# A graph layer on one core: sixteen groups of the first norm ahead of the tables with eight load buffers, the densest groups in twos, the last layer's dense pair due 100 slots before its end

## The chip, the cores and the metric

The kernel runs on one core of a Trainium2 chip. The metric is the device time of one execution in microseconds (us), and shorter is better. Before the change three runs gave 6620.86, 6623.79 and 6653.34 us, a median of 6623.79. One further execution was taken by the profiler; all durations below come from it.

## The reference

There are 12500 nodes with 256 features each and 200000 edges (`src`, `dst`), sorted by `dst`. `dst` is drawn as a square of a uniform number, so that low nodes have many edges. Cut to what matters:

```python
xn = layernorm(x)
h = xn
for l in range(3):                        # three graph layers
    s = segment_sum(h[src], dst); cnt = segment_sum(1, dst)
    h = (s / max(cnt, 1)) @ Wl[l].T + bl[l] + h @ Wr[l].T
    h = leaky_relu(h, 0.01) if l < 2 else log_softmax(h)
x = x + h + linear_attention(xn)          # 4 heads of 32
t = layernorm(x)                          # top 2 of 8 experts, softmax router
out = x + t + sum(comb[:, e] * (gelu(t @ w1[e] + b1[e]) @ w2[e] + b2[e]) for e in range(8))
```

Every layer therefore needs the complete result of the layer before, since an edge may start at any node.

## The kernel before, in words

**Tiling.** The nodes are cut into 98 blocks of 128 (`NB`). Blocks are numbered from the end by `r`: r = 97 is block 0, the one with the most edges. The list `falling` holds groups of consecutive blocks in the order in which they are worked, from r = 0 up: 23 groups of four (`G`), then r 92 to 95 as one group of four and r 96 to 97 as one of two, 25 in all. `FEWER` is 92, `MORE` is 96. The edges of a block are cut into slots of at most 128 edges; a table `due` gives the slot at which block r is complete at the latest, 1240 for r = 91 and 1404 for r = 95.

**The start** (L275 to L604). Instructions of this part are placed by a scheduler that goes by data dependences and gives priority to what the program writes earlier. (1) Edge numbers are loaded in chunks into `val`, whether they are sorted is tested, and `val` is written to a table `edges` in device memory (L411). (2) `first_norm` (L279) normalizes one group: load `xt` on SP's DMA queue (L176), statistics on DVE (L228, L229), a root on ACT (L231), the norming on ACT (L289), a store to `y` on ACT's DMA queue (L291). The first `EARLY` = 10 groups are written ahead of the test and the write of `edges`, the other 15 behind the tables. Four buffers hold loads (`xt`), three hold results (`o_norm`). (3) The tables say for each slot which nodes its 128 edges start at (`src_of`) and which node of the block they end at (`dst_of`): samples of `edges` (L427), a gather `near` (L444), the slot ends, `pack` for the three densest pairs of blocks with 33 comparing passes each (`junk`, L532), and 13 rounds that gather 128 edge rows, turn them on TensorE and copy them (L577 to L601, tile `got`, two buffers).

**The three layers** (`on_the_way`, L1072). From here on the order of instructions is the order in which the program writes them. In layers 0 and 1 each slot has a gather by POOL of 128 rows of `y` (L1380), a one-hot matrix made by DVE for four slots at a time (L1372), and a matmul on TensorE that adds one-hot x messages to the block's sums in `acc` (L1399). When a block's slots are over, `take_up` (L1410) scales its sums on DVE and clears them; when the last block of a group is taken up, the group's `products` (L669) are queued: in layer 0 its transposes (`turned`, L661 and L663) and the product with Wl (`p_l`, L679), then transposes and the linear step of the next layer (`linear`, L240: `p_mm` L247, additions L257, for layer 2 also the three bf16 parts L268 and L269, stores of `y` and `z`). The six densest blocks, r 92 to 97, take no slots in layers 0 and 1: a count matrix of each pair of blocks, made in layer 0, is multiplied with all rows of `y` (`sums`, L1308, matmul L1330), spread evenly up to slot `sums_to`. Layer 2 does so only for r 96 and 97 (`LAST` = 1); the other blocks have slots there, and messages travel as three bf16 parts, three matmuls per slot.

`load_z` (L1451) brings a group's half-made `z` of the next sum. It lies in one of three buffers `h` of four blocks; only the last group, of two blocks, has a buffer `h_c` of its own in layers 0 and 1.

**Experts in layer 2.** When a group has its sums, DVE finishes `z`, SP stores it (L1448), and the group is `ready`. `softmaxed` (L807) loads it again (L812, L814), takes log-softmax (maximum L819, exponentials and logarithm on ACT), the norm (L228 to L237), transposes (L661), the router (L847), the top two and `comb` (to L879), its transpose (L883) and the product with `b2` (L892). `expert_steps` (L908) runs the eight experts of a group (`p_h` L975, Gelu L977, `p_y` L944, weighing L931), and between these steps lets the next ready group's `softmaxed` go on one step, once the group before has been stored (L902). The steps are let in slot by slot by a credit in the loop of `on_the_way_of` (L1351): 1.12 us per slot, less 0.6 for each step of `sums`. What is left when the slots are over runs after them, in the same order.

Of the kernel before, what the change touches and what calls it, by code (L numbers as in the profile page):

```python
# [41 lines left out]
F32 = mybir.dt.float32  # L42
# [13 lines left out]
P = 128  # L56
D = 256
# [5 lines left out]
G = 4  # L63
# [2 lines left out]
RING, SHARED = (4, 6, 4), (1, 2, 2)  # L66
W = D + 1
AHEAD = 8
EARLY = 10
MSGS, PARTED = 32, 24  # L70
FEW = 4
HOTS = 3
# [1 line left out]
PAIRS = 3  # L74
# [12 lines left out]
def gps_kernel(ctx: ExitStack, tc: tile.TileContext, x, src, dst, wlr, bl, wq, wk, wv,  # L87
# [4 lines left out]
    NB = (N + P - 1) // P  # L92
# [6 lines left out]
    FEWER = NB - DENSE  # L99
    MORE = NB - 2 * LAST  # L100
    falling, group_of = [], []
    for r0, r1 in ((0, FEWER), (FEWER, NB)):
        for r in range(r0, r1, G):
            n = min(G, r1 - r)
            group_of.extend([len(falling)] * n)
            falling.append((NB - r - n, n))
    NG = len(falling)
# [62 lines left out]
    def rows(t, b, n):  # L170

        return t[b * P:(b + n) * P, :].rearrange("(j p) d -> p j d", p=P)

    def load_x(t, b, n):
        if b + n < NB or tail == P:
            nc.sync.dma_start(t[:, :n, :], rows(x, b, n))  # L176
            return
        nc.vector.memset(t, 0.0)
        if n > 1:
            nc.sync.dma_start(t[:, :n - 1, :], rows(x, b, n - 1))  # L180
        nc.sync.dma_start(t[:tail, n - 1, :], x[N - tail:N, :])
# [41 lines left out]
    def norm_stats(pool, t, n):  # L223

        st = pool.tile([P, G, nc.vector.BN_STATS_DIM], F32, name="st")
        mv = pool.tile([P, G, nc.vector.BN_AGGR_DIM], F32, name="mv")
        for j in range(n):
            nc.vector.bn_stats(st[:, j, :], t[:, j, :])  # L228
            nc.vector.bn_aggr(mv[:, j, :], st[:, j, :])  # L229
        rs = pool.tile([P, G], F32, name="rs")  # L230
        nc.scalar.activation(rs[:, :n], mv[:, :n, 1], AF.Sqrt, bias=eps)  # L231
        return mv, rs
# [41 lines left out]
    with ExitStack() as first:  # L274
        sort = first.enter_context(tc.tile_pool(name="sort", bufs=1))  # L275
        work = first.enter_context(tc.tile_pool(name="work", bufs=2))
        psum = first.enter_context(tc.tile_pool(name="psum1", bufs=1, space=PSUM))

        def first_norm(b, n):  # L279
            xt = work.tile([P, G, D], F32, name="xt", bufs=4)  # L280
            load_x(xt, b, n)
            o = work.tile([P, G, D], F32, name="o_norm", bufs=3)
            mv, rs = norm_stats(work, xt, n)
            nc.vector.reciprocal(rs[:, :n], rs[:, :n])
            less = work.tile([P, G], F32, name="less_mean")
            nc.vector.scalar_tensor_tensor(less[:, :n], mv[:, :n, 0], -1.0, rs[:, :n],
                                           op0=OP.mult, op1=OP.mult)
            for j in range(n):
                nc.scalar.activation(o[:, j, :], xt[:, j, :], AF.Identity, bias=less[:, j:j + 1],  # L289
                                     scale=rs[:, j:j + 1])  # L290
            nc.scalar.dma_start(rows(y_tab[0], b, n), o[:, :n, :])  # L291
# [111 lines left out]
        for t, w in ((wq_sb, wq), (wk_sb, wk), (wv_sb, wv), (wo_sb, w_out)):  # L403
            nc.scalar.dma_start(t, w)
        for b, n in falling[:EARLY]:
            first_norm(b, n)
# [18 lines left out]
        for c in range(KC):  # L425
            n = min(P, NK - c * P)
# [57 lines left out]
        for s0 in range(0, NS, 512):  # L484
            n = min(512, NS - s0)
# [116 lines left out]

        for b, n in falling[EARLY:]:
            first_norm(b, n)  # L604
# [467 lines left out]
    def on_the_way():  # L1072


        with ExitStack() as stack:
# [14 lines left out]
            with ExitStack() as two:  # L1090
                msgs = take_messages(open_pool(two, "messages"), MSGS)
                for layer in range(2):
                    with ExitStack() as own:
                        psum = open_pool(own, f"psum_w{layer}", space=PSUM)
                        on_the_way_of(layer, tables[layer], due[FEWER - 1], work, psum, inv, msgs,
                                      a, Counts(own), None)
# [6 lines left out]
            c = Counts(stack)  # L1103
            c.work = open_pool(stack, "sums2")
            on_the_way_of(2, where, due[MORE - 1], work, psum, inv, msgs, a, c, e)

    class Counts:
# [243 lines left out]
    def on_the_way_of(layer, table, last, work, psum, inv, msgs, a, c, e):  # L1351
# [7 lines left out]
        hots, made_of, cleared, taken, zs, at, at_of = {}, {}, {}, {}, {}, (), -1  # L1359
# [90 lines left out]

        def load_z(g):  # L1451
            b, n = falling[g]
            if g == NG - 1 and not e:
                zs[g] = c.work.tile([P, G, D], F32, name="h_c")
            else:
                zs[g] = work.tile([P, G, D], F32, name="h", bufs=3)
            nc.sync.dma_start(zs[g][:, :n, :], rows(z_tab[layer], b, n))

        def ask(g):

            while layer == 0 and g not in made:
                stage(1)
            load_z(g)
# [47 lines left out]
        n_steps = (LAST if e else PAIRS) * (NB + 6) + 3  # L1511
        if layer == 0:
            counting = c.all_counted(psum, whole, inv)
        sums_to = last - 40
        due_steps, done_steps = 0.0, 0
        credit, r, g = 0.0, 0, 0
        nc.vector.memset(acc, 0.0)
# [138 lines left out]
```

## Time and profile before

| what | value |
|---|---|
| runs | 6620.86, 6623.79, 6653.34 us (median 6623.79) |
| profiled execution, its own time | 6628.48 us |
| its span (1.8 us less) | 6626.7 us |
| granted TensorE clock, mean | 0.903 |
| busy: TensorE, weight loads | 5213.0 us (79%), 3776.3 us |
| busy: VectorE (DVE), ScalarE (ACT), GpSimd (POOL) | 2590.6, 1025.2, 4076.9 us |
| start, to the first gather of layer 0 | 202.4 us |
| last gather of layer 0, first of layer 1 | 2472.3, 2514.5 us |
| last gather of layer 1, first of layer 2 | 4323.7, 4350.5 us |
| last product of a slot, end | 6527.4, 6626.7 us |

How to read it: the page cuts the span into 40 slices of 165.7 us and gives each engine's busy tenths in them. The chain of waits is followed back from the last instruction, at each step to what released it. In a timeline each row has a start, a duration, the engine (PE is TensorE, PEld its weight loads, SPq and ACTq are DMA issues), the line of the kernel, the operation, out<-in by the program's names, and in brackets the idle time of the engine before it with what ended it.

### The profile page before, as it was taken

The page shows a single profiled execution, that of the slowest core. Times are in us where ns is not written, and L with a number is a line of the kernel's source. Part 1 is how long each engine was busy: PE and PEld are TensorE (multiplying, and loading weights), DVE is VectorE, ACT ScalarE, POOL GpSimd, SP SyncE. Part 2 cuts the span into 40 slices and gives each one's busy share as a digit, 9 for nine tenths or more (in the row PEclk, how much of TensorE's full clock was granted, in tenths as well). Part 3 has the DMA queues.
Part 4 walks back from the last instruction along what each step waited for, and adds up shares of the span by engine and source line. Part 5 has one row for each costly group of instructions (what it writes and reads, how often), then busy time and mean ns, then how long its engine had stood idle before and what let it go on. Part 6 is the DMA issues. An engine that isn't in the chain of part 4 may idle for free.

```text
span 6626.7 us, 73745 instructions
## 1 busy us (share of the span) xinstructions
PE 5213.0 (79%) x23854; PEld 3776.3 (57%) x23854; DVE 2590.6 (39%) x7080; ACT 1025.2 (15%) x1884; POOL 4076.9 (62%) x4146
## 2 busy tenths in 40 slices
PE   1467779777888886777777666549999999999997
PEld 0346656555666664555555445426666666666665
DVE  6425747566412112333322221124444444444442
ACT  2111111111100000000000000002222222222221
POOL 1565566665566665667666666646666666666661
PEclk9879989899999898888888877769999999999998
DMA  5544434444566655666665555445666555556551
GB/s 157 148 116 141 150 105 143 119 135 141 173 216 215 214 183 182 219 207 213 206 202 180 153 160 163 135 156 165 180 180 179 176 176 166 174 168 179 161 158 56
DMA packets 711084, 1101.56 MB, mean 166 GB/s; under 512 B 105392, under 2 KB 548806, under 8 KB 710460
## 3 DMA queue, kind: packets, MB, share of 16 engines
q0 software_dynamic: 213712, 604.20, 31.8%
q1 hardware_dynamic: 479455, 472.47, 22.1%
q10 hardware_dynamic: 17546, 20.04, 0.9%
q8 instruction: 220, 3.60, 0.2%
q14 instruction: 151, 1.24, 0.1%
HBM read 908.22 MB, written 188.11 MB: 165 GB/s over the span
## 4 chain that ended last, share of the span: by engine, by line
PE 53%; another core or an unknown queue 13%; issue 7%; DVE 6%; POOL 2%; DMA 1%; ACT 1%; SPq 0%; DVEq 0%; ACTq 0%; POOLq 0%
PE acc L1399 17%; PE p_h L975 10%; PE p_y L944 9%; PE whole L1330 7%; PE p_mm L247 4%; POOL msg L1380 2%; PE p_n L1231 1%; PE p_tr L661 1%; PE p_a L801 1%; DVE hots L1372 1%; DVE src_hot L1211 1%; PE p_b L892 1%; DVE dst_hot L1213 1%; PE p_r L847 1%
## 5 line engine op out<-in xcount | busy, mean ns | idle before, releaser
L1380 POOL DMA_INDIRECT msg<-y,src_of x2480 | 2519.0, 1016 | 1467.9 <-issue 655.5
L1399 PE MATMUL acc<-msg,hots 128*128 128x257 f32 (+1 forms) x4960 | 1426.9, 415 | 657.8 <-DVE inv_w L1423 225.7
L1380 POOL DMA_INDIRECT msg_parts<-y_parts,src_of x1404 | 1403.3, 999 | 778.9 <-issue 350.3
L1399 PEld LDWEIGHTS acc<-msg,hots 128*128 128x128 f32 x4960 | 988.2, 207 | 932.2 <-issue 307.6
L1372 DVE TENSOR_TENSOR hots<-cols,dst_of 128x512 f32<-128x512 f32 (+1 forms) x971 | 662.4, 688 | 1524.3 <-PE acc L1399 763.7
L1330 PE MATMUL whole<-y_c,count 128*128 128x256 f32 x2744 | 763.3, 399 | 86.0 <-issue 68.1
L975 PE MATMUL p_h<-turned,w_sb 128*128 128x512 f32 (+1 forms) x1600 | 756.6, 596 | 24.0 <-issue 12.6
L944 PE MATMUL p_y<-w_sb,hT 128*128 128x256 f32 x3136 | 747.5, 381 | 5.7 <-ACT hT L977 3.1
L1399 PE MATMUL acc<-msg_parts,hots 128*128 128x256 bf16 x4212 | 630.4, 277 | 44.0 <-issue 21.0
L1330 PEld LDWEIGHTS whole<-y_c,count 128*128 128x128 f32 x2744 | 543.5, 201 | 180.9 <-issue 93.5
L1399 PEld LDWEIGHTS <-hots 128*128 128x128 bf16 x4212 | 415.4, 100 | 380.3 <-issue 282.1
L944 PEld LDWEIGHTS p_y<-w_sb,hT 128*128 128x128 f32 x3136 | 569.8, 191 | 83.7 <-issue 10.7
L931 DVE SCALAR_TENSOR_TENSOR x<-p_y,comb,x 128x256 f32<-128x256 f32 x784 | 340.8, 476 | 513.8 <-PE p_y L944 249.2
L247 PE MATMUL p_mm<-wlr_sb,turned 128*128 128x512 f32 x784 | 382.7, 633 | 128.7 <-DVE yz L261 74.5
L663 ACT COPY turned<-p_tr 128x512 f32<-128x512 f32 (+1 forms) x250 | 138.2, 580 | 2174.3 <-PE p_tr L661 1342.3
L977 ACT ACTIVATE hT<-p_h,b_sb 128x512 f32<-128x512 f32 (+1 forms) x400 | 269.6, 679 | 1220.6 <-PE p_h L975 640.7
L975 PEld LDWEIGHTS p_h<-turned,w_sb 128*128 128x128 f32 x1600 | 279.9, 194 | 227.2 <-issue 208.0
L257 DVE TENSOR_TENSOR yz<-p_mm,bl_sb 128x256 f32<-128x256 f32 x196 | 81.3, 423 | 688.7 <-issue 297.2
L247 PEld LDWEIGHTS p_mm<-wlr_sb,turned 128*128 128x128 f32 x784 | 157.0, 203 | 300.4 <-issue 267.0
L1211 DVE TENSOR_SCALAR src_hot<-nums,source_of 128x384 bf16<-128x384 uint16 x693 | 224.1, 323 | 208.3 <-remote 75.6
L1231 PE MATMUL p_n<-dst_hot,src_hot 128*128 128x256 bf16 x2058 | 278.3, 285 | 29.9 <-issue 20.5
L1231 PEld LDWEIGHTS <-src_hot 128*128 128x128 bf16 x2058 | 207.3, 102 | 94.2 <-issue 44.5
(301 smaller groups left out, 3837.3 us busy)
## 6 DMA issues: line engine op xcount, KB each, us to landing
count<-counts SPq DMA_DIRECT2D x294, 256.0 KB
y_c<-y SPq DMA_DIRECT2D x294, 256.0 KB
msg<-y,src_of POOLq DMA_INDIRECT x2480
h<-z SPq DMA_DIRECT2D x72, 512.0 KB
counts<-counts_sb SPq DMA_DIRECT2D x96, 384.0 KB
z<-yz SPq DMA_DIRECT2D x98, 256.0 KB
msg_parts<-y_parts,src_of POOLq DMA_INDIRECT x1404
y_parts<-y SPq DMA_DIRECT2D x49, 384.0 KB
```

The costliest lines, as they stand in the source:

```text
L247: nc.tensor.matmul(p, hT[:, k, j * P:(j + 1) * P], w[:, k, :], start=(k == 0), stop=(k == 1))
L663: nc.scalar.copy(tT[:, k, :n * P], p_tr[:, :n * P])
L931: nc.vector.scalar_tensor_tensor(xt[:, j, :], p[:, j - j0, :], comb[:, j, i:i + 1], xt[:, j, :], op0=OP.mult, op1=OP.add)
L944: nc.tensor.matmul(p[:, j - j0, :], hT[:, k, j * P:(j + 1) * P], e.w2[:, i, k, :], start=(k == 0), stop=(k == 1))
L975: nc.tensor.matmul(p_h[:, :n * P], e.w1[:, i, k, m * P:(m + 1) * P], tT[:, k, :n * P], start=(k == 0), stop=(k == 1))
L977: nc.scalar.activation(hT[:, m, :n * P], p_h[:, :n * P], AF.Gelu, bias=e.b1[:, i, m:m + 1])
L1211: nc.vector.tensor_scalar(src_hot[:, i, :], self.nums, source[:, c:c + 1], None, op0=OP.is_equal)
L1231: nc.tensor.matmul(p[:, t, :], s_hot[:, (t0 + t) * P:(t0 + t + 1) * P], d_hot, start=(i == 0), stop=(i == len(mine) - 1))
L1330: nc.tensor.matmul(acc[:, h * D:(h + 1) * D], c[:, j, h * P:(h + 1) * P], y[:, j, :], start=False, stop=True, skip_group_check=True)
L1372: nc.vector.tensor_tensor(hot[:, :n, :], cols.rearrange("p (o c) -> p o c", o=1).to_broadcast([P, n, P]), dst_of[:, s:s + n].rearrange("p ...
L1380: got = nc.gpsimd.indirect_dma_start(out=msgs[s % held] if e else msgs[s % held][:, :D], out_offset=None, in_=y_parts if e else y_tab[laye ...
L1399: got = nc.tensor.matmul(sums, hot, msgs[s % held][:, k * D:k * D + w], start=False, stop=True, skip_group_check=True)
```

## The change

Five edits: `EARLY` from 10 to 16; buffers of `xt` from four to eight; the last ten blocks (r 88 to 97) in groups of two where there were groups of four and one of two, which makes 27 groups; in layers 0 and 1, the three dense groups (r 92 to 97) get a buffer `h_c` of two blocks each; in layer 2 the summing of the pair r 96, 97 ends 100 slots ahead of the last slot, where it was 40. The diff, whole:

```diff
@@ -66,7 +66,7 @@
 RING, SHARED = (4, 6, 4), (1, 2, 2)
 W = D + 1
 AHEAD = 8
-EARLY = 10
+EARLY = 16
 MSGS, PARTED = 32, 24
@@ -99,9 +99,10 @@
     FEWER = NB - DENSE
     MORE = NB - 2 * LAST
     falling, group_of = [], []
-    for r0, r1 in ((0, FEWER), (FEWER, NB)):
-        for r in range(r0, r1, G):
-            n = min(G, r1 - r)
+    SMALL = FEWER - 4
+    for r0, r1, most in ((0, SMALL, G), (SMALL, NB, 2)):
+        for r in range(r0, r1, most):
+            n = min(most, r1 - r)
             group_of.extend([len(falling)] * n)
             falling.append((NB - r - n, n))
@@ -277,7 +278,7 @@
         def first_norm(b, n):
-            xt = work.tile([P, G, D], F32, name="xt", bufs=4)
+            xt = work.tile([P, G, D], F32, name="xt", bufs=8)
             load_x(xt, b, n)
@@ -1450,8 +1451,8 @@
         def load_z(g):
             b, n = falling[g]
-            if g == NG - 1 and not e:
-                zs[g] = c.work.tile([P, G, D], F32, name="h_c")
+            if g >= group_of[FEWER] and not e:
+                zs[g] = c.work.tile([P, 2, D], F32, name="h_c", bufs=PAIRS)
             else:
                 zs[g] = work.tile([P, G, D], F32, name="h", bufs=3)
@@ -1511,7 +1512,7 @@
         n_steps = (LAST if e else PAIRS) * (NB + 6) + 3
         if layer == 0:
             counting = c.all_counted(psum, whole, inv)
-        sums_to = last - 40
+        sums_to = last - (100 if e else 40)
```

## The prediction

> **What bounds the kernel now.** I read the page first: its slices and its chain of waits.
>
> ```profile
> PE   1467779777888886777777666549999999999997
> PEclk9879989899999898888888877769999999999998
> ...
> PE 53%; another core or an unknown queue 13%; issue 7%; DVE 6%; POOL 2%; DMA 1%; ACT 1%; SPq 0%; DVEq 0%; ACTq 0%; POOLq 0%
> ```
>
> A slice is 165.7 us. TensorE leads the chain, and from slice 27 on (layer 2) it is full; layers 0 and 1 run at 5 to 8 tenths. Slice 1 shows one tenth: the start, without TensorE. So I read the stages apart, by the first and last gathers in POOL's timeline: start to 202.4, layer 0 to 2514.5, layer 1 to 4350.5, layer 2 slots to 6527.4, tail to 6626.7. The change touches the start, the seams and the tail.
>
> The start, from the busy time by windows (PE, PEld, DVE, ACT, POOL, clock, DMA share, GB/s):
>
> ```profile
> 35.00:55.00 20.00, 0.00 (x0) 0.00 (x0) 5.07 (x30) 4.82 (x11) 0.00 (x0) 1.00 0.59 203
> 80.00:110.00 30.00, 10.13 (x23) 1.54 (x23) 28.65 (x223) 3.84 (x9) 1.68 (x3) 1.00 0.27 89
> 110.00:150.00 40.00, 6.03 (x22) 2.72 (x22) 27.47 (x183) 15.03 (x45) 9.46 (x10) 1.00 0.39 114
> 170.00:200.00 30.00, 0.00 (x0) 0.00 (x0) 10.61 (x59) 16.92 (x37) 0.00 (x0) 1.00 0.81 257
> ```
>
> DVE is full only from 80 to 110 (pack's 99 passes of 0.32 us, 31.5 us). From 170 to 200 nothing of the tables is left: norms alone, on the DMAs. The timeline there:
>
> ```profile
> 163.14 0.94 POOL L591 DMA_INDIRECT got<-edges,of_i  x1 [5.88 <-ACT o_norm L289]
> ...
> 196.97 0.37 ACTq L291 DMA_DIRECT2D y<-o_norm  x1
> ...
> 202.38 1.31 POOL L1380 DMA_INDIRECT msg<-y,src_of  x1 [38.29 <-DMA y<-o_norm]
> ```
>
> The last table piece lands at 166.0 and is turned by 167.6, yet the first gather waits until 202.4 for the norms' stores, as it reads rows of any block. That is the wait which ends last: 34.8 us behind the tables.
>
> **The change, part by part.**
>
> *The first norms: 10 to 16 groups ahead, 4 to 8 loads.* A group of four costs DVE four statistics 0.54 us apart and two small ones, 2.3 us, ACT 2.07 for four normings and 0.3 for the root, 2.4 us, and 1 MB read and written, 4 us at 257 GB/s. The number of instructions is the same (two blocks more per group aside); they are moved. Now ten stores are issued by 87.6, then none until 121.3, since DVE is in pack and an SP load stood 34 us (87.59 to 121.31) for one of four buffers. With 16 ahead, six more groups take 14 us of DVE in 35 to 80, where it is busy 21 of 45; with eight buffers the next loads already lie there when pack ends. Eleven groups remain (27 in all), and of the 15 that remain now seven are stored between 110 and 168. Four more need 9 us of DVE and 10 of ACT; DVE idles 12.5 + 10.6 us in 110 to 170. So the norms come off the end and **the tables are late next**. They move too: their chain of edge chunks, edge write, samples, near, pack and 13 table rounds loses some 5 us to the four additional loads (2 MB of the 257 GB/s is 8 us, part of it in idle DMA), gains 5 where samples no longer stand in SP's queue behind loads that wait for buffers (53.55 to 66.0 now), and loses 4.6 to two more groups' DVE work near pack. The first round, now at 114.5, is then between 114 and 118; the rounds take 45 to 52 us as now, so tables end at 165 to 172 and the first gather is at 171 to 178. I take 176: **-26**. Cover: if the norms still end last I lose it all but 4; if the rounds quicken (the first pair took 6.5 us, the mean 8.2), it is -40. Range -40 to -4. DVE's first one-hot pass (200.8 to 212.8) moves along.
>
> *Layers 0 and 1: last groups of two, z of three groups kept apart.* The last products of a layer run with no slots left beside them.
>
> ```profile
> 4323.67 0.95 POOL L1380 DMA_INDIRECT msg<-y,src_of  x1 [0.30 <-issue]
> 4350.45 2.34 POOL L1380 DMA_INDIRECT msg_parts<-y_parts,src_of  x1 [25.83 <-DMA z<-yz]
> ```
>
> With two blocks instead of four behind layer 1's last slot, 8 of 16 turned-and-multiplied pieces go, by the first and second linear pass 4339.9 to 4344.9 and its transposes: -6.0. Layer 0: p_mm 16 to 8 (-3.4) and p_l 16 to 8 (-1.7), -5.3 with copies. But the two blocks' products, 12.1 us of TensorE per group of four, go into the slots, where TensorE is mostly the bound: +5 and +3.5; and more groups are more waits, +2 each at most. The loads of z are more and smaller (three of 0.25 MB instead of one of 0.5 and one of 0.25), issued early, off the path. A fourth "h" holder costs nothing but memory. Sum: -11.3 + 8.5 + 1 = **-2**, range -10 to +6.
>
> *Layer 2: groups of two, the dense pair done 100 slots from the end.* The order of the work is a rule of the program (experts' steps are let in by a credit of 1.12 us per slot, less 0.6 per summing step), so I followed it slot by slot. Now the experts of group 96-97 are through near slot 1397, the last slots' 21 products stand alone (second row below), and the last group of four is ready only with the last slot. TensorE's timeline:
>
> ```profile
> 6517.15 1.03 PE L975 MATMUL p_h<-turned,w_sb 128*128 128x256 f32 x4
> ...
> 6524.91 2.46 PE L1399 MATMUL acc<-msg_parts,hots 128*128 128x256 bf16 x21
> 6546.58 1.39 PE L661 MATMUL p_tr<-ident,o 128*128 128x128 f32 x4 [19.21 <-DVE o L237]
> ...
> 6558.18 0.37 PE L883 MATMUL p_c<-ident,comb 128*32 128x128 f32 x1 [4.16 <-DVE comb L879]
> ...
> 6563.75 8.06 PE L975 MATMUL p_h<-turned,w_sb 128*128 128x512 f32 x12
> ```
>
> From 6527.4 to 6563.75 the softmax chain is open: 36.3 us with TensorE idle for 25.9; then 55 us of experts and the last store, 99.3 us in all behind the last slot. After: the counts give the groups of two as ready at slots 1179, 1230 (the dense pair, by the 100), 1239, 1311 and 1403. The last is again ready only at the end, with half the chain's work; the group before it still has its experts to run and, as its host, covers part of the chain. Work before the last slot falls by 6.5 us (1903.6 to 1897.0 by count) and that behind it rises from 57.9 to 64.4: no gain in sum. What the cover is worth: a chain from the store to the first p_tr, by the one hosted by a group of two,
>
> ```profile
> 6407.21 0.38 SPq L902 DMA_DIRECT2D out<-x  x1
> 6411.23 0.36 SPq L812 DMA_DIRECT2D x<-xa_tab  x1
> 6411.64 0.46 SPq L814 DMA_DIRECT2D o<-z  x1
> ```
>
> reached p_tr at 6427.77, 20.5 us; its rows without waits (landing 4.0, load 4.4, exponentials, logarithm, norms) sum to 17. A host of two blocks gives TensorE 11 us until then with slots, 7.5 in the tail; a host of four gave 22 to 27. So three hosts of two stall 6 us each, 18, where now gaps are 0 to 2.9; the tail stalls 9.5 + 3 and is slow for 4 more. Before the last slot: 18 - 6.5 = +11.5 to +13.5; the tail: 64.4 + 9.5 + 3 + 4 + the end's 2 = 83 to 84.5 instead of 99.3: -15. **-2**, range -14 (chain half hidden) to +14 (20.5 each and a full stall at the end). By itself, the 100 moves the dense group 60 slots earlier and changes neither count nor tail: 0. TensorE's rate for two blocks is unhurt: four 256-column p_h start 0.87 us apart, of 512 columns 1.72.
>
> **Sum:** -26 - 2 - 2 = -30. On the profiled execution (6628.5; span 6626.7 and 1.8 around it) 6598.5; the median shown is 6623.8, 4.7 less, so **6594 us**.
>
> **The rivals.**
>
> *B, the tables run free*: with norms ahead, rounds go 6.5 us a pair, first gather at 162, and hosts of two stall 2 us each instead of 6, 12 less: -40 - 2 - 14 = -56: 6568. For it: DVE's idle time after 110. Against: near and pack are DVE's. 0.22.
>
> *C, hosts pay the full 20.5 us* (the +14 above) and the seams' work comes back with 2 more: -26 + 2 + 14 = -10: 6614. For it: the only host of two seen took 20.5. Against: it ran among slots, with waits that are not the chain's. 0.16.
>
> *D, the loads stand before the tables*: SP issues both, in one queue; eight loads ahead are 4.2 MB, 2.1 more than now, 8 us at 257 GB/s. Each of the tables' six dependent SP trips (three chunks, edges, samples, pair) could wait that long: 48 us, the first gather at 221 (+19), with -4 for the rest +15: 6639. It decides once the tables lengthen by over 31 us. Against: the stores that free buffers before 60 are 2 to 14 us apart, so no trip finds the whole 4.2 MB ahead of it. The Trainium skill, "DMA: Bandwidth & Descriptors", section "Queues, rings and completion order", says that each SDMA engine takes the descriptors of a ring in order, and SP has one row; by that rule D's mechanism exists, and the trace agrees in that samples were issued over 12 us among loads, but shows no price beyond it. 0.10.
>
> *E, weight loads show*: in groups of two, each p_h has half the columns per weight load; 64 more loads of 0.194 us would add 12.4 if nothing hid them: 6606. Against: the 0.87 of the row above. The Trainium skill, "TensorE: Matmul & The Clock Gate", section "The mechanism" (of Part 3), says weight loads overlap running matmuls only when their row groups differ; by that they would show here, and the rows do not. 0.02.
>
> *F, the order does not change at the start* (the loads stay behind the tables): -4 - 2 - 2, 6616. 0.04.
>
> **How the numbers follow.** A, the forecast, 0.46, own range 6575 to 6612; B 0.22 (6555 to 6583); C 0.16 (6605 to 6625); D 0.10 (6620 to 6665); E 0.02; F 0.04. From 6560 to 6630 leaves out a quarter of B (0.06) and most of D (0.07): 0.13, with A's tails under 0.2. About 0.5% (33 us) is what a measurement of this kernel can tell: under 6591 lie B and four tenths of A, 0.40; over 6657 a quarter of D and an unknown, 0.04; the rest 0.56.
>
> **What would show it.** First gather at 176 (not 202), released by a table round instead of y's store; loads of xt between 35 and 80 without a wait of 34 us; layer 1's seam 20 instead of 26.8 us; from the last slot to the end 83 instead of 99.3; p_tr in layer 2's last 300 slots behind gaps of 6. Wrong if the gather comes after 195, or a table round begins after 130.

## The result, and the profile after

The changed kernel ran in 6590.58 us, the median of seven runs (6574.54 to 6616.33); the kernel before, on the same chip, in 6635.23, the median of seven (6599.28 to 6657.99). The ratio, estimated from all these runs, is 0.995, with a 95% interval from 0.9927 to 0.9973: some 33 us less (the two medians alone differ by 44.7). On another chip, where the same pair was run once more in an experiment below, the ratio was 0.9983 (0.9962 to 1.0004, which does not exclude that nothing was gained; the medians there differ by 28.3 us). The two intervals overlap only between 0.9962 and 0.9973, so the gain is best read as 0.2 to 0.5%. The forecast was 6594 us, 30 us less.

The profiled execution took 6608.92 us, its span is 6607.1 (before 6626.7). The first reading is again the page's slices and its chain:

```profile
PE   1557778787888886777866756549999999999998
PEclk9888989899999987888888877769999999999999
...
PE 59%; another core or an unknown queue 12%; issue 10%; DVE 9%; DMA 3%; POOL 3%; ACT 2%; SPq 0%; ACTq 0%; DVEq 0%; POOLq 0%
```

TensorE has still one tenth in the first slice, but more in the second; the clock is as before. Where the time went is read from stages, cut by the first gather of each layer, the start of the last take-up of a layer's sums, and the last product of a slot:

| stage (us) | before | after | difference |
|---|---|---|---|
| start, to layer 0's first gather | 202.4 | 184.4 | -18.0 |
| layer 0, to the last take-up | 2292.9 | 2270.7 | -22.2 |
| take-up to layer 1's first gather | 19.2 | 13.3 | -5.9 |
| layer 1, to the last take-up | 1815.3 | 1832.5 | +17.2 |
| take-up to layer 2's first gather | 20.6 | 14.7 | -5.9 |
| layer 2's slots | 2176.9 | 2207.8 | +30.9 |
| tail | 99.3 | 83.6 | -15.7 |

The start, by windows, with the columns as before:

```profile
35.00:55.00 20.00, 0.19 (x2) 0.09 (x2) 12.14 (x65) 7.08 (x16) 0.00 (x0) 1.00 0.68 220
...
80.00:110.00 30.00, 9.39 (x17) 1.31 (x17) 26.62 (x167) 12.57 (x29) 1.68 (x3) 1.00 0.68 213
110.00:150.00 40.00, 5.45 (x24) 2.33 (x24) 33.21 (x264) 15.90 (x43) 7.58 (x8) 1.00 0.41 131
```

The largest change is in the last column of 80 to 110: the DMAs moved 213 GB/s, where it was 89. That is 30 us x 124 GB/s = 3.7 MB, nearly four groups of the norm (1 MB each), which used to stand at the end, at 257 GB/s some 15 us. DVE was hardly emptier there than before (26.6 of 30 us, where it was 28.7). The gathers of the start, from POOL's timeline:

```profile
124.82 0.96 POOL L592 DMA_INDIRECT got<-edges,of_i  x1 [24.92 <-DVE of L583]
...
168.75 0.95 POOL L592 DMA_INDIRECT got<-edges,of_i  x1 [4.39 <-ACT src_of L602]
184.41 1.75 POOL L1381 DMA_INDIRECT msg<-y,src_of  x1 [14.72 <-DVE where L1082]
```

The first table round comes at 124.8 (before 114.5), the last at 168.7 (before 163.1), and the first gather 15.7 us behind it instead of 39.2. The gather's row names DVE's `where` as the last releaser; but the norms are late as well: the store issued last, on ACT's queue, is one of theirs, and in the experiments start and best, with the same two edits of the start but one small group instead of five, the first gather's releaser is "DMA y<-o_norm".

```profile
181.30 0.37 ACTq L292 DMA_DIRECT2D y<-o_norm  x1
```

Layer 2's end has gained waits that were not there before (TensorE's timeline):

```profile
6399.25 2.07 PE L976 MATMUL p_h<-turned,w_sb 128*128 128x256 f32 x4 [5.38 <-ACT hT L978]
...
6451.97 2.08 PE L976 MATMUL p_h<-turned,w_sb 128*128 128x256 f32 x4 [5.66 <-ACT hT L978]
...
6505.10 2.08 PE L976 MATMUL p_h<-turned,w_sb 128*128 128x256 f32 x4 [6.24 <-ACT hT L978]
...
6547.73 2.08 PE L976 MATMUL p_h<-turned,w_sb 128*128 128x256 f32 x4 [5.61 <-ACT hT L978]
6550.40 0.75 PE L662 MATMUL p_tr<-ident,o 128*128 128x128 f32 x2 [0.59 <-PE p_h L976]
```

Four waits of 5.4 to 6.2 us, the last in the tail (slots end at 6523.5). In return the tail's 36 us of open softmax chain are gone: TensorE idles 6 us in it, where it idled 26. What stands before such a wait is seen in all engines' timeline around the first of the four:

```profile
6384.78 0.38 SPq L903 DMA_DIRECT2D out<-x  x1
...
6388.61 0.36 SPq L813 DMA_DIRECT2D x<-xa_tab  x1
...
6389.06 0.42 SPq L815 DMA_DIRECT2D o<-z  x1
...
6392.52 1.03 PE L976 MATMUL p_h<-turned,w_sb 128*128 128x256 f32 x4
...
6393.32 0.69 DVE L820 TENSOR_REDUCE low<-o 128x2 f32<-128x512 f32 x1 [2.40 <-DMA o<-z]
6393.37 1.28 ACT L825 ACT_TABLE_LOAD   x1 [2.63 <-DMA o<-z]
...
6394.66 0.51 ACT L825 ACTIVATE ex<-o,low 128x256 f32<-128x256 f32 x1
...
6395.91 1.28 ACT L827 ACT_TABLE_LOAD   x1
...
6397.43 1.28 ACT L978 ACT_TABLE_LOAD   x1
...
6398.73 0.84 ACT L978 ACTIVATE hT<-p_h,b_sb 128x256 f32<-128x256 f32 x2
...
6399.25 2.07 PE L976 MATMUL p_h<-turned,w_sb 128*128 128x256 f32 x4 [5.38 <-ACT hT L978]
```

The group whose experts run is called the host, the next one, whose softmax chain goes on between them, the guest. The host's Gelu for the p_h of 6392.52 stands in ACT's order behind the guest's exponentials and logarithm. ACT had idled 2.63 us for the guest's `o`, issued at 6389.06, but that has landed by 6393.32, and the p_h ends at 6393.55; so what the Gelu waits for is ACT's own work, 5.36 us from 6393.37 to 6398.73, of which three table loads (for the exponential, the logarithm and the Gelu) are 3.84. TensorE has nothing else meanwhile. In the second and fourth wait too the load has landed by the time the p_h ends (to 0.1 us), in the third 0.6 us after it.

### The profile page after: what moved, and what is told of

Its sections match the earlier page's. It is cut to its first block, busy times and chain, and to the rows that moved or that the text cites. A ratio compares the mean times of both kernels' runs of the same rounds, so it can differ in the third digit from the quotient of the medians.

```text
span 6607.1 us, 74238 instructions
## 1 busy us (share of the span) xinstructions
PE 5214.3 (79%) x23992; PEld 3805.8 (58%) x23992; DVE 2597.2 (39%) x7130; ACT 1058.9 (16%) x1970; POOL 4064.5 (62%) x4146
## 4 chain that ended last, share of the span: by engine, by line
PE 59%; another core or an unknown queue 12%; issue 10%; DVE 9%; DMA 3%; POOL 3%; ACT 2%; SPq 0%; ACTq 0%; DVEq 0%; POOLq 0%
PE acc L1400 19%; PE p_h L976 9%; PE p_y L945 9%; PE whole L1331 7%; PE p_mm L248 4%; POOL msg L1381 3%; PE p_n L1232 3%; PE p_tr L662 2%; DVE hots L1373 2%; PE p_a L802 1%; PE p_l L680 1%; DMA o<-z 1%; DVE src_hot L1212 1%; PE whole L1236 1%
## 5 line engine op out<-in xcount | busy, mean ns | idle before, releaser
L976 PEld LDWEIGHTS p_h<-turned,w_sb 128*128 128x128 f32 x1728 | 305.5, 195 | 238.9 <-issue 192.9
```

The source lines that it names most:

```text
L976: nc.tensor.matmul(p_h[:, :n * P], e.w1[:, i, k, m * P:(m + 1) * P], tT[:, k, :n * P], start=(k == 0), stop=(k == 1))
```

## The experiments

Twelve kernels were run, four on each of three chips, each four beside runs of the kernel before on the same chip (medians 6630.0, 6691.25 and 6687.45 us), so ratios are compared, not times. A single execution differs from its kernel's median by some 20 us, at times by 40 to 50, and the stages of a profile vary with it: late100's profile is the slowest of its twelve executions, 36 us above their median, and pref's lies 36 below. The stages are therefore read over all profiles. "4" and "2" say whether the last groups are as before or of two.

| kernel | start | layer 0 | seam | layer 1 | seam | layer 2 | tail | ratio (95%) |
|---|---|---|---|---|---|---|---|---|
| before (4) | 202.4 | 2292.9 | 19.2 | 1815.3 | 20.6 | 2176.9 | 99.3 | 1 |
| start (4) | 181.1 | 2274.8 | 19.2 | 1813.7 | 20.6 | 2184.0 | 99.4 | 0.9969 (0.9949 to 0.999) |
| early (4) | 188.6 | 2298.8 | 19.2 | 1840.1 | 20.3 | 2207.0 | 98.2 | one run |
| bufs (4) | 192.3 | 2293.1 | 19.2 | 1840.7 | 21.0 | 2198.1 | 99.4 | one run |
| late100 (4, 100) | 202.6 | 2279.5 | 19.2 | 1836.0 | 20.2 | 2225.8 | 98.5 | 1.0018 (0.9998 to 1.0038) |
| ownz (4) | 203.5 | 2320.1 | 19.2 | 1841.1 | 18.9 | 2200.0 | 99.4 | 1.0005 (0.9987 to 1.0023) |
| dense2 (dense 2) | 206.6 | 2304.4 | 20.5 | 1834.2 | 18.5 | 2200.1 | 72.5 | 0.9989 (0.9967 to 1.0012) |
| twos (2) | 206.4 | 2255.8 | 15.0 | 1836.2 | 14.6 | 2199.8 | 79.4 | 0.9977 (0.9958 to 0.9996) |
| after (2, 100) | 184.4 | 2270.7 | 13.3 | 1832.5 | 14.7 | 2207.8 | 83.6 | 0.995 (0.9927 to 0.9973) |
| again (2, 100) | 183.2 | 2279.7 | 13.3 | 1835.0 | 14.7 | 2249.3 | 83.3 | 0.9983 (0.9962 to 1.0004) |
| pref (2, 100) | 185.5 | 2275.7 | 15.0 | 1829.6 | 14.5 | 2225.3 | 81.8 | 0.9947 (0.9924 to 0.997) |
| four2 (2 in layers 0 and 1, 4 in layer 2, 100) | 183.9 | 2265.8 | 13.3 | 1829.3 | 13.0 | 2198.5 | 99.9 | 0.9978 (0.996 to 0.9997) |
| no100 (2) | 186.1 | 2270.4 | 13.3 | 1849.9 | 14.5 | 2220.9 | 80.7 | 0.9923 (0.99 to 0.9946) |
| best (2) | 182.6 | 2297.1 | 13.1 | 1857.8 | 14.0 | 2227.1 | 79.0 | 0.9943 (0.9922 to 0.9964) |

### The parts alone: start, twos, late100

**start**, the kernel before with

```diff
-EARLY = 10
+EARLY = 16
-            xt = work.tile([P, G, D], F32, name="xt", bufs=4)
+            xt = work.tile([P, G, D], F32, name="xt", bufs=8)
```

> The kernel before with only the two edits of the start (16 groups ahead, eight load buffers). Theory: the start alone gives what the changed kernel's start gave, first gather at 184 instead of 202.4 us, and everything behind it is as before: last products of layers 0 and 1 within 10 us of the lengths before (2293 and 1814 us from first gather to last take-up), layer 2 2177 us of slots and a tail of 99. Time ratio 0.997, -18 us. Rival 1: layer 0's first slots wait for something else and give the 18 us back, ratio 0.999 to 1.000. Rival 2: the early norms lengthen the tables by over 31 us, ratio above 1.000.

Measured: first gather 181.1, ratio 0.9969. Layers, seams and tail are those of the kernels with "4". The start keeps its gain to the end; rival 2 falls, and of rival 1 only the value 0.999 lies at the edge of the interval.

**twos**, the kernel before with the new `falling` and `load_z` of the diff.

> The kernel before with only the groups of two and the own z buffers. Theory: from the last take-up to the next layer's first gather 13.3 us instead of 19.2 (layer 0) and 15.6 instead of 21.6 (layer 1); layers 0 and 1 up to the take-up lengthened by the work moved into them, +5 and +3.5 us, +2 for waits; layer 2's slots 2177 + 17 (three or four waits of 5.4 to 6.2 us at p_h for a Gelu) and a few more, the tail 84 instead of 99. In sum -12 + 10 + 25 - 15 = +8, ratio 1.001. Rival: the own z buffers free layer 0 and the 22 us that it lost in the changed kernel belong to this edit: -14, ratio 0.998.

Measured: ratio 0.9977. The seams are 15.0 and 14.6, the tail 79.4, and there are waits of 6.7, 3.8 and 5.6 us at p_h. The sum was expected at +8 and came out at -15: layer 0 is not 7 us longer but 37 shorter than in the one profile of before. Its rival, the own z buffers, is taken up below (ownz). The start is 4.0 us longer, which the prediction had not counted: five groups of two at the end of the first norm instead of two of four and one of two.

**late100**, the kernel before with

```diff
-        sums_to = last - 40
+        sums_to = last - (100 if e else 40)
```

> The kernel before with only the 100 slots instead of 40. Theory: nothing, 0 within 5 us, ratio 1.000: the last group of four is ready only with the last slot as before, tail 99. Rival: the summing steps, denser by 4.6%, take the experts' credit in the slots and lengthen layer 2 by 10 to 15 us as the middle slots of the changed kernel (300 to 1000) were 16 us longer: ratio 1.002.

Measured: 1.0018, at the edge of what can be told; layer 2's slots 2225.8, in a profile of a slow execution. The theory of no effect does not hold for the order of the work. The rival's number came, but with a wait that it had not named; whether its credit takes part is not shown. The dense pair's group of two now comes ahead of group r 88 to 91, and is host to its chain (SP, DVE and TensorE rows of all engines' timeline):

```profile
6456.90 0.46 SPq L814 DMA_DIRECT2D o<-z  x1
...
6463.79 1.22 DVE L819 TENSOR_REDUCE low<-o 128x4 f32<-128x1024 f32 x1 [7.71 <-DMA o<-z]
...
6470.98 2.07 PE L975 MATMUL p_h<-turned,w_sb 128*128 128x256 f32 x4 [9.53 <-ACT hT L977]
```

The host's p_h has 256 columns (two blocks), the guest's `o` 1024 (four): its load takes 6.9 us to the maximum, 2.7 of them after the host's p_h has ended, then ACT works 6.6 us up to the Gelu (four exponentials instead of two), and TensorE waits 9.5. In the kernel before this group had no guest.

### Where layer 2's time goes: four2, pref, no100

**four2**, the changed kernel with the groups of before in layer 2 alone:

```diff
+        falling, group_of = groups(((0, FEWER, G), (FEWER, NB, G)) if e else
+                                   ((0, SMALL, G), (SMALL, NB, 2)))
```

> The changed kernel, but layer 2 takes its groups as before (four blocks, the last of two). Theory: layer 2's slots go back to 2177 us without the waits of 5.4 to 6.2 us at p_h, and its tail to 99; start 184 and the shorter seams stay. Against the changed kernel -31 + 16 = -15, ratio to the kernel before 0.9925 to 0.996. Rival: most of the 31 us that layer 2's slots gained in the changed kernel are not of the groups of two (a profile's spread, or the 100): slots stay near 2200, tail 99, ratio 0.997 to 0.999.

Measured: 0.9978, slots 2198.5, tail 99.9. These are the rival's numbers: the 2177 us of the one profile of before was low, since the kernels with the old groups and 40 take 2177 to 2207. This kernel has the 100 too, and with it one wait of 11.8 us as in late100.

**pref**, the changed kernel with other empty steps in the softmax chain of a group of two:

```diff
-        yield 0.0
-        yield 0.0
-        yield 0.0
+        for _ in range(8 if n == 2 else 3):
+            yield 0.0
         low = work.tile([P, G], F32, name="low")
...
-        for _ in range(4):
+        for _ in range(3 if n == 2 else 4):
...
-        for _ in range(3):
+        for _ in range(2 if n == 2 else 3):
...
-        for _ in range(5):
+        for _ in range(3 if n == 2 else 5):
```

> The changed kernel with the steps of the softmax chain of a group of two spread otherwise: eight empty steps instead of three between its loads and its maximum, and four fewer further behind. Theory: the p_h waits of 5.4 to 6.2 us come from a Gelu that stands in ACT's queue behind an exponential which waits for the loaded z; with the exponential issued later they go, four times, -15 to -20 us in layer 2's last 200 slots and tail: ratio 0.992 to 0.993. Rival: the wait moves on to p_tr or p_r of the same guest, as the chain is 17 us long whatever is issued when: ratio 0.995, waits of 4 to 6 us at p_tr or p_b.

Measured: 0.9947, as the changed kernel (0.995, on another chip). The waits at p_h are gone, and these have come (TensorE's timeline):

```profile
6427.92 0.75 PE L662 MATMUL p_tr<-ident,o 128*128 128x128 f32 x2 [5.00 <-issue]
...
6479.40 0.84 PE L662 MATMUL p_tr<-ident,o 128*128 128x128 f32 x2 [4.77 <-issue]
...
6532.06 0.61 PE L662 MATMUL p_tr<-ident,o 128*128 128x128 f32 x2 [3.62 <-issue]
...
6574.02 0.75 PE L662 MATMUL p_tr<-ident,o 128*128 128x128 f32 x2 [5.26 <-issue]
```

The rival holds: the chain from the load to p_tr is longer than the work of a host of two, whatever is issued when. Issuing the exponentials later only moved the wait to another row.

**no100**, the changed kernel with `sums_to = last - 40`.

> The changed kernel without the 100 (40 as before). Theory: the 100 alone made the kernel before slower by 0.18% because the dense pair's group of two now comes ahead of another group and is host to its softmax chain, with a wait at p_h of 9.5 to 11.8 us where the guest has four blocks; in the changed kernel all late guests have two, and the waits are 5.4 to 6.2 each: without the 100 one of them goes, 4 to 10 us, ratio to before 0.993 to 0.9945. Rival: with groups of two the place of the dense pair does not matter, 0.995 as the changed kernel.

Measured: 0.9923 (on another chip than the two measurements of the changed kernel, 0.995 and 0.9983, with an interval that overlaps the first). That is below the theory's range, and the rival's 0.995 lies just outside the interval. In the last slots and the tail two waits at p_h exceed 2.5 us, 5.3 and 5.7, where the changed kernel had four in each of its profiles (5.4, 5.7, 6.2, 5.6 and, in again, 9.1, 5.4, 2.9, 5.7). But the number of hosts did not fall, as the theory had it: no100 has four of two blocks as well, with the same work of ACT, and behind two of them TensorE had other products to do and idled only 2.1 and 1.3 us. Why is not shown.

### The start apart: early, bufs

**early** has only `EARLY = 16`, **bufs** only `bufs=8`.

> The kernel before with 16 groups ahead but four load buffers, for its start alone. Theory: the order gives most of the 21 us of both edges, since the six groups then stand ahead of pack in DVE's order; but each load behind the fourth waits for a buffer and the rest of the norms is late again: first gather at 188 (both edges 181.1, neither 202.4). Rival: without buffers nothing comes earlier, 198 or more, as the loads that stand in SP's queue hold the tables' samples up.

> The kernel before with eight load buffers but ten groups ahead, for its start alone. Theory: four more loads lie ready when pack ends, so the norms behind it are not held by loads; but nothing more is done ahead of pack: first gather at 193. Rival: the buffers alone do it, 181 to 185, and the order of the program is without effect.

Measured: 188.6 and 192.3, close to the theories' 188 and 193. Each edit alone gives half to two thirds: -13.8 and -10.1, both together -21.3. POOL's timelines, early first, then bufs:

```profile
124.84 0.96 POOL L591 DMA_INDIRECT got<-edges,of_i  x1 [19.91 <-DVE of L582]
```

```profile
111.04 0.96 POOL L591 DMA_INDIRECT got<-edges,of_i  x1 [18.64 <-DVE of L582]
```

The tables' first round is late by the order (124.8), not by the eight loads: with these alone it comes at 111.0, 3.5 us earlier than before.

### Why layer 0 is shorter: ownz, dense2

**ownz**, the kernel before with

```diff
-            if g == NG - 1 and not e:
-                zs[g] = c.work.tile([P, G, D], F32, name="h_c")
+            if g >= group_of[FEWER] and not e:
+                zs[g] = c.work.tile([P, G, D], F32, name="h_c", bufs=2)
```

> The kernel before with only a z buffer of its own for both dense groups (four blocks each, two buffers), so that the three buffers h are free for the others. Open is why layer 0, from its first gather to its last take-up, took 2256 to 2276 us in the five profiles with groups of two and 2275 to 2299 in the five without (means 2268 and 2288). Theory: a dense group of four kept one of the three buffers h through the summing, and the other groups' z loads came late; with own buffers layer 0 is at 2268 here, ratio 0.997. Rival: it is the smaller last groups; layer 0 stays near 2288, ratio 1.000.

**dense2**, the kernel before with twos (and their z buffers) for r 92 to 97 alone.

> The kernel before with groups of two only for the dense blocks (r 92 to 97), each with its z buffer; r 88 to 91 stay one group of four. Theory: seams of 19.2 and 20.5 us as before, since the last group by slots in layers 0 and 1 has four blocks; layer 2's tail 80 to 84 instead of 99, as the last group has two; layer 0 at 2268 if own z buffers or the dense groups' size carry the 20 us. Rival: layer 0 near 2288, so the 20 us belong to r 88 to 91. Ratio 0.997 by the theory, 0.999 to 1.001 by the rival.

Measured: layer 0 took 2320.1 and 2304.4 us, ratios 1.0005 and 0.9989. In both the rival's numbers come: neither the own z buffers nor the dense groups' size made layer 0 shorter in its one profile, and ownz's interval excludes the theory's 0.997 (dense2's just includes it). The shorter layer goes with r 88 to 91 in two groups. Besides, dense2's tail is 72.5, even shorter than expected, and its slots and tail together, 2272.6 us, are the shortest of all fourteen profiles; no kernel here has its groups in layer 2 together with r 88 to 91 in twos in layers 0 and 1. Over all profiles layer 0 to its take-up is 2294.8 us on average in the seven kernels without that and 2273.6 in the seven with it. Of these 21 us, 6 lie behind the last gather: TensorE is then 18.2 us behind on average, and 12.0 with groups of two, in every one of them less (10.5 to 13.0 against 15.1 to 23.0). For the other 15 the cause is open, and the spread between profiles is about as large. TensorE's busy time in layer 0 is the same in both sets (1815 and 1817 us on average); what is shorter is its idle time, 480 us without and 457 with. The largest difference is at acc, in the waits for DVE's `inv_w`, the first step of a take-up, up to the last gather: 207 us on average without and 182 with, but the ranges overlap (170 to 226 and 171 to 200), and smaller waits elsewhere are longer.

### Without the 100 and the small norms: best, again

**best**, no100 with the first norm in groups of four throughout, whatever `falling` has:

```diff
+    norms = [(NB - r - min(G, NB - r), min(G, NB - r)) for r in range(0, NB, G)]
...
-        for b, n in falling[:EARLY]:
+        for b, n in norms[:EARLY]:
```

> The changed kernel without the 100, and with the first norm in groups of four throughout (25 instead of 27). Theory: the five small groups at the end of the first norm cost 3 to 4 us of the start (first gather 184 to 186 with them, 181 without): first gather at 181 to 182, ratio to before 0.9915 to 0.993. Rival: the start is set by the last table round (landing at 173) and not by the norms: 184 to 186 as in the changed kernel, ratio 0.9925.

**again** is the changed kernel itself.

> The changed kernel once more, on the chip of the three others, to stand beside the one without the 100. Theory: the 100 costs: ratio to before 0.994 to 0.996, 0.2% or more above the kernel without it. Rival: both are equal within 0.1%, and the lower ratio without the 100 was the spread between chips.

Measured on one chip: best 0.9943 (first gather 182.6), again 0.9983 (183.2), both ratios above what was expected. The kernel without the 100, its norms in fours besides, is ahead by 0.4% by the ratios and 0.2% by the medians here, and no100 was ahead of the first measurement of the changed kernel by 0.27%, from chip to chip; the intervals just touch on this chip, so it is likely, not certain, that the 100 costs time. Best still has three waits at p_h, 9.4, 3.5 and 5.5 us. The small groups of the norm cost 0.6 to 3.5 us (183.2 to 186.1 in the five others with both edits of the start and all small groups, 182.6 here).

## Why the prediction was right, and where its steps failed

**The sum** was right (-30 forecast, -33 and on another chip -11 measured by ratio), but partly by luck, because errors in three terms cancelled. With the stages of the result for the start, the means over the profiles for the rest: start -18 (forecast -26), seams and layers 0 and 1 together -26 (forecast -2), layer 2 some +18 (forecast -2), in sum -26.

**The start** (-26 forecast, -18.0 measured, -21.3 alone). Two steps failed. The first is "six more groups take 14 us of DVE in 35 to 80": by 80 eight norms had been stored, as before. The six were stored between 92 and 118, their DVE work done between pack's passes, which ended at 121.8 instead of 111.6, and so the first table round came at 124.8 instead of 114 to 118. DVE's idle time in 35 to 80 was no measure: the DMAs moved 222 GB/s there before and 220 after, and only 4 us of DVE work more went in; that the DMAs were the limit is likely, not shown.

The second is "four more" norms beside the table rounds, with "the norms come off the end": six were stored between 118 and 170, as six were before between 121 and 165. DVE idled 15.7 us between 122 and 170, but 12.7 of them it waited for the rounds' own gathers with the rest of its work in order behind. So five norms were left, and they still end last, their last store 8 us behind the landing of the tables at about 173. "If the norms still end last I lose it all but 4" did not hold either: the gain comes from the DMA time in 80 to 110 that lay idle, so that five norms of two blocks are left at the end where there were nine of four (one of two).

**Rival D** (loads ahead of the tables in SP's queue) is refuted by bufs, where the rounds come earlier with eight loads (111.0 instead of 114.5). By the Trainium skill, "DMA: Bandwidth & Descriptors", section "Queues, rings and completion order", descriptors of one ring are taken in order; no run shows a price of that here.

**The seams** (-6.0 and -5.3): measured -5.9 each from the last take-up on, right. The sign put on record, 20 us from layer 1's last gather to layer 2's first, did not come: it was 27.6 (26.8 before), as the last take-up stood 12.8 us behind the last gather in this profile, 6.1 before; over all profiles that lag is 9.2 us on average with the new groups and 8.4 without. Of the moved work, layer 1 measured +7 (means 1831.6 and 1838.6 us, with a spread of 11 between profiles), which agrees with the forecast of +5.5 but could be nothing; layer 0 measured -21 instead of +7. The step "TensorE is mostly the bound" in layer 0 failed: TensorE idles there for 442 to 494 us of 2256 to 2320 in all profiles, so moved work need not lengthen it. The 6 us less behind the last gather are shown, the rest is open.

**Layer 2.** The tail was right in size (-15 forecast, -15.7 measured), though its one wait is 5.6 us where the prediction had put 9.5 + 3. The size of a host's wait was right as well (6 forecast, 5.4 to 6.2 measured), but it stands at p_h and not at p_tr: the prediction had not seen that the guest's exponentials and logarithm, with their table loads, stand ahead of the host's Gelu on ACT.

The step that failed is "the 100 ... changes neither count nor tail: 0". With the old groups it makes the dense group a host, with a wait of 9.5 to 11.8 us; with groups of two the waits over 2.5 us at p_h sum to 22.9 and 23.1 us with the 100 (the changed kernel and again) and to 16.1, 11.0 and 18.4 with 40 (twos, no100 and best). Slots and tail together took 2292.4 us on average in the kernels with the old groups and 40 (five profiles, 2276 to 2305), 2295.6 with twos and 40 (three, 2279 to 2306), but 2310.4 (three, 2292 to 2333) and 2311.4 (two, 2298 to 2324) with the 100. So groups of two cost 3 us in sum, near the forecast of -2, and the 100 some 15 to 19, of which the waits at p_h account for about half. The ranges overlap, and the two longest profiles, late100 and again, also have the lowest granted clock in layer 2 of all fourteen (0.946 and 0.948, the others 0.953 to 0.961). So the price of the 100 is likely, and its size is not settled.

**Rival C** (hosts pay 20.5) is out with the measured waits. Its row had been misread: the chain of 6407.21 is not that of a host of two. Its guest has two blocks, but its host's p_h have 512 columns, and the one group of two, which ran from 6476.7 to 6526, had no guest. **Rival B** is out too: the table rounds took 44 us from first to last, where it had 39, and the first gather came at 184, not 162. **Rival E** had counted 64 more weight loads at p_h, and there are 128 (1600 and 1728 matmuls on the two pages). It is refuted all the same by the changed kernel's tail, where there are no slots to hide a load. The first two rows are from it, the third is from the kernel before:

```profile
6534.19 1.89 PE L976 MATMUL p_h<-turned,w_sb 128*128 128x256 f32 x8
6535.91 1.89 PE L945 MATMUL p_y<-w_sb,hT 128*128 128x256 f32 x8
```

```profile
6573.37 1.88 PE L975 MATMUL p_h<-turned,w_sb 128*128 128x512 f32 x4
```

Eight matmuls of 256 columns, with twice the weight loads per column, take 1.89 us; four of 512 took 1.88. The rule of the Trainium skill, "TensorE: Matmul & The Clock Gate", section "The mechanism", that weight loads overlap matmuls only where row groups differ, does not hold for these rows.

## What to carry to other kernels

Idle time of the engine that computes is not room for more work where the DMAs are already busy, or where the engine waits for a chain with its other work in order behind: ask in each window what the idle time waits for, and move work to where all that it needs is free. A smaller last group shortens the end, but as a host it also hides less of the next group's chain; count the chain (an estimated 17 us here, the sum of its rows) against the host's work. A due time that only moves a small group earlier can change what stands behind it.

## What the runs showed of the hardware that was not expected

Work of ACT for one group held up a ready Gelu of another that stood behind it: two exponentials and a logarithm took 5.36 us of ACT, four and a logarithm 6.6, and TensorE idled 5.4 to 6.2 us for the first. Each change of function adds a table load of 1.28 us in the rows, so three of them are 3.84 of the 5.36 us. Where the load of the guest had not landed when the p_h ended, that came on top: 2.7 us with 0.5 MB in late100, for 9.5 in all. One kernel's runs on one chip differed by up to 82 us (6635.19 to 6716.86, 35 runs of the kernel before), and the kernel before's medians by 61 us between chips, which is more than the effects measured; ratios on one chip were needed for all of them.
